# A two-layer scan kernel: carried states copied by VectorE instead of GpSimd, with three smaller edits

## The chip, the cores and the metric

The kernel runs on one core of a Trainium2 chip. Such a core has five engines with an instruction queue each: TensorE (PE in the profile), VectorE (DVE), ScalarE (ACT), GpSimd (POOL) and SyncE (SP, which here issues the transfers). Each engine works through its queue in order, and semaphores make an instruction wait for work on another engine. The metric is the device time of the whole launch in microseconds (us). The kernel before takes 21017.66 us, the median of three runs that lie between 21011.35 and 21024.16.

## The reference: two state-space layers

The input is a batch of 8 images of 48 x 48 positions with 192 channels. Each layer normalises it by groups, runs a selective scan over it, and adds the result to its input. Layer 0, which alone is changed, widens to 384 channels, runs a 3 x 3 convolution by channel, and scans every image in four directions `k`: by rows, by columns, and both of them backwards. Layer 1 scans single rows and columns forwards and backwards.

```python
xs = jnp.stack([xr, xc, jnp.flip(xr, -1), jnp.flip(xc, -1)], axis=1)
def step(h, inp):
    ut, dtt, bt, ct = inp
    dA = jnp.exp(dtt[..., None] * A)
    h = dA * h + (dtt * ut)[..., None] * bt[:, :, None, :]
    y = jnp.einsum('bkdn,bkn->bkd', h, ct)
    return (h, y)
y = ys[:, 0] + col2row(ys[:, 1]) + jnp.flip(ys[:, 2], -1) + col2row(jnp.flip(ys[:, 3], -1))
```

In words: for each of 384 channels and 16 states a first-order recurrence runs along 2304 positions. `dtt` is a softplus of a small projection, `bt` and `ct` are projections shared by the channels. The outputs of the four directions are added, normalised over the channels, multiplied by a gate `z`, and projected back to 192 channels.

## The kernel before

**Tiles.** The 384 channels are three groups `j` of 128 partitions. A direction's 2304 positions are cut into six chunks of 384. One chunk of one direction of one image is an *item*; layer 0 has 8 x 4 x 6 = 192 of them, and layer 1 as many. An item has 16 states `n` with three channel groups each, so 48 scan instructions of 128 x 384. The three scans of one state share a tile `h` of 128 x 1152; call them a *group*. Layer 0 has 3072 groups.

**One group on the engines.** ScalarE computes the decays `a = exp(dt * A)` (line 435), one per channel group. For most states a product `bT = dtu * B` is made, either by ScalarE in three instructions (line 464) or by GpSimd in one (line 459), and TensorE transposes it into a PSUM tile `b` (line 512, three banks in turn). For states 4 and 11 of layer 0 (`DIAGONAL`) a diagonal matrix `db` is made from B instead, by ScalarE in three instructions (line 483) or by GpSimd in one (line 480), and TensorE multiplies with it (line 503). For state 8 VectorE multiplies in PSUM (line 523). VectorE then scans: `h` from `a` and `b` (line 1059). GpSimd multiplies the whole `h` tile by `C`, in place (line 548, called the *gather* here). TensorE transposes and sums the result over the states into `y` (line 565). Four `h` tiles are in use in turn.

**The carried state.** A direction's chunks follow each other, so a scan starts from the last value of the chunk before it. After the three scans of a group, the last column of `h` (the first, for a reversed direction) is copied into a small tile `carry`, 128 x 3 elements (lines 541 to 544 ask for it, `put_carry`, line 1027, emits it, and the profile gives it line 1030). GpSimd does this copy immediately before its gather of the same tile, since the gather overwrites `h`. Every chunk but the last of a direction has it: 160 items x 16 = 2560 copies.

**What sets the order.** Nothing is scheduled at run time. Generators (`decays`, `weighs`, `matrices`, `places`, `scans`, `gathers`, `adds`, and others for the projections) yield a `Need`: a due time counted in scans, a cost for each engine that may do it, and what must precede it. `Plan.run` picks, with its own clock of assumed costs, the engine and the need that can start first, and among those ready the one due first; `late` adds to the due time on one engine. So an assumed cost decides which engine gets a step and where in that engine's queue it stands. Where only one engine has a cost, that engine always does it.

**Around the scans.** `enters` projects the items in pairs (due between `lo` and `hi`, in scans before the item's own) and `block` applies softplus to them. `products` forms `du = dt * u` on GpSimd (line 372). `finish` adds an item's output to `acc` on VectorE. `tails` normalises, gates and projects `acc` by chunks of eight rows, while the last direction of the image runs: after the add of the last direction's chunk `c`, it reads rows 8c to 8c + 7. In the kernel before, the last direction is `k = 3`, reversed columns, whose chunk `c` is eight columns over all rows.

Of the kernel before, what the change touches and what calls it, by code (L numbers as in the profile page):

```python
# [25 lines left out]
NJ = 3  # L26
# [7 lines left out]
NSEG = N * NJ  # L34
# [5 lines left out]
PE, DVE, ACT, POOL, SP = "PE", "DVE", "ACT", "POOL", "SP"  # L40
# [8 lines left out]
LATE = 3  # L49
# [34 lines left out]
class Plan:  # L84
# [11 lines left out]
    def mark(self, *key):  # L96
        return self.marks.setdefault(key, Mark())
# [85 lines left out]
class Common:  # L183
# [217 lines left out]
    def stream(self, plan, pool, items, direct, diagonal, decay, scan, finish, held, kept, weighed):  # L401
# [11 lines left out]
        nc, mark = self.nc, plan.mark  # L413
# [54 lines left out]
        def matrices():  # L468
            for i, item in enumerate(items):
                for n in sorted(diagonal):  # L470
                    after = [mark("bt", i)]
                    if placed:
                        after += [mark("place", placed[-1] + j) for j in range(NJ)]
                    need = Need(i * NSEG + NJ * n - 6, {POOL: 0.8, ACT: 0.72}, after, sets=[mark("matrix", i, n)])
                    yield need
                    to = dbs[i, n] = pool.tile([P, TB, P], F32, tag="db", name="db", bufs=1)
                    by = item["bt"][:, :, R + n : R + n + 1]
                    if need.e == POOL:
                        of = self.ident.unsqueeze(1).to_broadcast((P, TB, P))
                        nc.gpsimd.tensor_tensor(to, of, by.to_broadcast((P, TB, P)), ALU.mult)  # L480
                    else:
                        for b in range(TB):
                            nc.scalar.activation(to[:, b, :], self.ident, AF.Copy, scale=by[:, b, :])
                    placed.append(i * NSEG + NJ * n)
# [50 lines left out]
        def gathers():  # L535

            for f in range(total // NJ):
                i, n = divmod(f, N)
                item = items[i]
                after = [mark("scan", NJ * f + j) for j in range(NJ)]  # L540
                if "carry" in item:
                    need = Need(NJ * f + 2.5, {POOL: 0.15}, after, sets=[mark("carry", i, n)])
                    yield need
                    item["carry"](need.e, n, hs[f])
                yield Need(NJ * f + 3, {POOL: 2.6}, after + [mark("cc", i, n // 2)], sets=[mark("gather", f)])
                h = hs[f]
                c = ccs[i, n // 2][:, n % 2, :].unsqueeze(1).to_broadcast((P, NJ, T))
                nc.gpsimd.tensor_tensor(h, h, c, ALU.mult)  # L548
# [56 lines left out]
        for lane in (fetches, decays, weighs, matrices, places, scans, gathers, adds):  # L605
            plan.start(lane())
# [4 lines left out]
def layer0(ctx, cm, x, xs, x2, w, norm):  # L611


    tc, nc = cm.tc, cm.nc
# [3 lines left out]
    mark = plan.mark  # L618
# [22 lines left out]
    carry = wp.tile([P, N * NJ], F32, name="carry")  # L641
# [2 lines left out]
    vs = [cm.dram.tile([P, NJ, L], F32, name=f"v{b}") for b in range(NIMG)]  # L644
    per = 4 * NC
    span = per * NSEG

    def piece(b, c, due, tag="xc", bufs=2, after=(), of=x):
        n = Need(due, {SP: 0.1}, after, lag=DMA)
        yield n  # L650
        xc = pool.tile([CP, NM, T], F32, tag=tag, name="xc", bufs=bufs)
        nc.sync.dma_start(xc, of[b][:, :, c * T : (c + 1) * T])
        return xc, n
# [213 lines left out]
    def enters():  # L867

        last = len(items) // 2
        gated = []
        for p in range(last + 1):
            b, q = divmod(p, per // 2)
            g = 2 * p
            lo, mid, hi = g * NSEG - 92, g * NSEG - 50, g * NSEG - 32
            if q < 3 and p < last:
                lo, mid, hi = g * NSEG - 56, g * NSEG - 46, g * NSEG - 30
                if q == 0 and b:
                    n = Need(lo - 10, {SP: 0.3}, [mark("du", g - 1), mark("v", b)], lag=9.0)  # L880
                    yield n
                    for i in range(3):
                        part = slice(i * L // 3, (i + 1) * L // 3)
                        nc.sync.dma_start(u[:, :, part], vs[b][:, :, part])
                after = [n] if b else [mark("conv", j, c) for j in range(NJ) for c in (2 * q, 2 * q + 1)]
                if q == 0 or b == 0:
                    yield from block(lo, after, thirds=[(b, q)])
            if p < last:
                pair = items[g : g + 2]
                after = yield from cm.project(plan, pool, p, pair, lo, mid, hi)  # L890
                thirds = [(b, q + 1)] if q < 2 and b else []
            else:
                pair, after, thirds = [], [], []
            ended = [g - 2, g - 1] if p and (g - 2) % per >= 3 * NC else []
            for i in ended:
                n = Need(hi - 20, {SP: 0.1}, [mark("z used", gated[-2])] if len(gated) > 1 else [], lag=DMA)
                yield n
                zts[i] = pool.tile([P, NJ, T], F32, tag="z", name="z", bufs=2)
                bi, r = divmod(i, per)
                cs = slice((NC - 1 - r % NC) * T, (NC - r % NC) * T)  # L900
                nc.sync.dma_start(zts[i], zs[bi][:, :, cs])
                gated.append(i)
                after = after + [n]
            if pair or ended:
                yield from block(hi, after, pair, thirds, ended)

    def block(due, after, pair=(), thirds=(), ended=()):

        tables = 1 + bool(pair) + bool(thirds or ended)
        cost = tables * TABLE + 1.07 * len(pair) + 2.05 * len(thirds) + 1.07 * len(ended)  # L910
        sets = [m for i in pair for m in i["softened"]]
        sets += [mark("u", *t) for t in thirds] + [mark("silu z", i) for i in ended]
        yield Need(due, {ACT: cost}, after, sets=sets)
        cm.softplus(pair)
        for _, q in thirds:
            part = slice(q * L // 3, (q + 1) * L // 3)
            nc.scalar.activation(u[:, :, part], u[:, :, part], AF.Silu)
        for i in ended:
            nc.scalar.activation(zts[i], zts[i], AF.Silu)
        cm.tables()  # L920
# [90 lines left out]
    def seen(t, j, k, c):  # L1011

        t, q = t[:, j, :], "" if type(j) is int else "j "
        order = f"p {q}(h w) -> p {q}h w" if k % 2 == 0 else f"p {q}(h w) -> p {q}w h"
        return t.rearrange(order, w=S)[..., c * RT : (c + 1) * RT, :]

    def by_rows(v, k):

        return v.rearrange("p w h -> p h w") if k % 2 else v

    def wanted(b, k, c):

        if k:
            return []
        return [mark("tail", b - 1, c)] if b else [mark("free")]

    def put_carry(e, q, h, rev):
        to, of = carry[:, q * NJ : (q + 1) * NJ], h[:, :, 0 if rev else T - 1]
        if e == POOL:
            nc.gpsimd.tensor_copy(to, of)  # L1030
        else:
            nc.scalar.copy(to, of)

    items = []
    for b in range(NIMG):
        for k in range(4):
            rev = k >= 2
            order = range(NC - 1, -1, -1) if rev else range(NC)
            for n, c in enumerate(order):
                item = dict(  # L1040
                    b=b, k=k, c=c, reverse=rev, carried=(n > 0), A=A[:, k],
                    wts=dict(xp=xp[:, k], dtw=dtw[:, k, :], dtb=dtb[:, k, :]),
                    u=lambda j, k=k, c=c: by_rows(seen(u, j, k, c), k), turned=k % 2,
                    all=seen(u, slice(None), k, c),
                    ready=[mark("u", b, q) for q in ((c // 2,) if k == 0 else range(3))],
                    cost=(0.7, 3.1 if k % 2 else 2.6, 0.915),
                    wanted=lambda j, b=b, k=k, c=c: wanted(b, k, c),
                )
                item["softened"] = [mark("dt", len(items))]
                if n < NC - 1:  # L1050
                    item["carry"] = lambda e, q, h, rev=rev: put_carry(e, q, h, rev)
                items.append(item)
# [28 lines left out]

    plan.start(prologues())
    plan.start(enters())
    plan.start(tails())
    cm.stream(plan, pool, items, DIRECT[0], DIAGONAL[0], decay, scan, finish, 4, 9, 3)
# [349 lines left out]
```

## Time and profile before

| what | value |
|---|---|
| median of three runs | 21017.66 us |
| the profiled execution, its own time | 21021.07 us |
| its span, first to last instruction | 21019.3 us |
| mean granted TensorE clock | 0.996 |
| layer 0, first scan to the last chunk | 109 to 10515 us |
| layer 1, scans | 10609 to 20999 us |
| busy over the span: PE, DVE, ACT, POOL | 96%, 94%, 96%, 95% |
| DMA, mean rate | 72 GB/s, transfers 22.8% of the 16 engines' span |

Each profile row names a line of the kernel, an engine, an operation, the tiles it writes and reads, and the count; then busy time and the mean of one instruction in ns; then the idle time of the engine ahead of these instructions and whose work ended it. All four compute engines are busy nearly all the time, so a row's share of busy time does not by itself say what sets the end.

### The profile page before, as it was taken

The numbers are of one execution on the slowest core, as the hardware profiler recorded it, in microseconds if no ns is written. First come the engines' busy times: TensorE is split into PE (matmuls) and PEld (weight loads), VectorE is DVE, ScalarE is ACT, GpSimd is POOL, SyncE is SP. The second block draws the span as 40 slices with busy tenths as digits, with TensorE's granted clock in tenths as the row PEclk, the third lists the DMA queues.
The fourth block names the chain that finished last, engine by engine and source line by source line (L and its number), as shares of the span: only waits on it lengthen the run. The fifth ranks groups of instructions, "written<-read, shape, count | busy, mean of one in ns | idle before, by whom it ended". The sixth has DMA issues, their size and how long they took to land.

```text
span 21019.3 us, 391720 instructions
## 1 busy us (share of the span) xinstructions
PE 20233.5 (96%) x138640; PEld 15731.1 (75%) x138640; DVE 19835.8 (94%) x25014; ACT 20092.6 (96%) x38482; POOL 19933.6 (95%) x10537
## 2 busy tenths in 40 slices
PE   9999999999999999998899999999999999999999
PEld 6777777777777777777767777777777777777777
DVE  7999999999999999999989999999999999999999
ACT  7999999999999999999989999999999999999999
POOL 7999999999999999999989999999999999999999
PEclk9999999999999999999999999999999999999999
DMA  2222222222222222222222222222222222222222
GB/s 78 76 87 72 87 72 76 87 73 85 75 76 88 72 87 75 74 79 64 71 61 65 65 65 65 65 65 65 66 67 67 68 67 68 68 68 67 68 69 66
DMA packets 728906, 1512.36 MB, mean 72 GB/s; under 512 B 181508, under 2 KB 324484, under 8 KB 726824
## 3 DMA queue, kind: packets, MB, share of 16 engines
q1 hardware_dynamic: 724768, 1485.21, 22.8%
q8 instruction: 1106, 18.12, 0.4%
q14 instruction: 848, 6.95, 0.1%
q10 hardware_dynamic: 2184, 2.08, 0.0%
HBM read 1382.03 MB, written 104.99 MB: 71 GB/s over the span
## 4 chain that ended last, share of the span: by engine, by line
PE 57%; DVE 17%; ACT 10%; POOL 9%; issue 6%; DMA 1%; DVEq 0%; POOLq 0%; SPq 0%; ACTq 0%
PE y L565 18%; PE b L512 17%; DVE h L1298 9%; POOL h L548 7%; PE dt_ps L344 4%; ACT bT L464 3%; DVE h L1059 3%; PE xd_ps L295 3%; PE cv_ps L767 3%; PE b L503 2%; PE o_ps L1333 2%; ACT l_da L435 2%; ACT a L435 2%; PE xi_ps L1190 2%; PE z_ps L1240 2%
## 5 line engine op out<-in xcount | busy, mean ns | idle before, releaser
L548 POOL TENSOR_TENSOR h<-h,cc 128x1152 f32<-128x1152 f32 x6144 | 16177.2, 2647 | 719.3 <-DVE h L1298 257.5
L1298 DVE TENSOR_TENSOR_SCAN h<-l_da,b 128x384 f32<-128x384 f32 x9216 | 8110.6, 934 | 234.3 <-PE b L512 160.0
L565 PE MATMUL y<-ident,h 128*128 128x128 f32 x55296 | 7673.2, 275 | 188.9 <-POOL h L548 175.3
L512 PE MATMUL b<-ident,bT 128*128 128x128 f32 x48384 | 7402.7, 276 | 339.2 <-DVE h L1059 162.9
L1059 DVE TENSOR_TENSOR_SCAN h<-a,carry,b 128x384 f32<-128x384 f32 x7680 | 7201.6, 994 | 413.5 <-PE b L512 215.5
L464 ACT ACTIVATE bT<-dtu,bt 128x384 f32<-128x384 f32 x13026 | 7518.3, 606 | 54.9 <-PE b L512 45.5
L565 PEld LDWEIGHTS y<-ident,h 128*128 128x128 f32 x55296 | 6273.8, 141 | 1621.5 <-POOL h L548 708.2
L512 PEld LDWEIGHTS b<-ident,bT 128*128 128x128 f32 x48384 | 5557.4, 141 | 2022.0 <-issue 629.0
L435 ACT ACTIVATE a<-dt,l_A 128x384 f32<-128x384 f32 x9216 | 5282.5, 607 | 166.3 <-DVE h L1059 152.8
L435 ACT ACTIVATE l_da<-dt,l_A 128x376 f32<-128x376 f32 x9216 | 5107.6, 600 | 36.0 <-DVE h L1298 33.8
L459 POOL TENSOR_TENSOR bT<-dtu,bt 128x1152 f32<-128x1152 f32 x1034 | 2188.4, 2118 | 43.8 <-PE b L512 34.0
L1059 DVE TENSOR_TENSOR_SCAN h<-a,b 128x384 f32<-128x384 f32 x1536 | 1357.3, 936 | 131.3 <-PE b L512 73.2
L372 POOL TENSOR_TENSOR du<-dt,u 128x1152 f32<-128x1152 f32 x384 | 1072.2, 2792 | 148.6 <-ACT dt L360 139.8
L344 PE MATMUL dt_ps<-xd,l_dtw 12*128 12x384 f32 x2304 | 1039.6, 533 | 11.9 <-DVE dt L231 3.2
L295 PE MATMUL xd_ps<-u,l_xp 128*44 128x384 f32 x2304 | 959.2, 505 | 21.9 <-DVE z L1305 13.9
L767 PE MATMUL cv_ps<-pad,diag 128*128 128x384 f32 x2376 | 951.2, 488 | 0.0
L1240 PE MATMUL z_ps<-xt,l_z 96*128 96x384 f32 x2304 | 919.9, 490 | 16.5 <-DVE u L1215 11.2
L503 PE MATMUL b<-db,dtu 128*128 128x128 f32 x6912 | 925.1, 279 | 10.0 <-DVE h L1059 9.3
L1333 PE MATMUL o_ps<-z,l_out 128*96 128x384 f32 x2304 | 921.0, 488 | 5.7 <-DVE z L1305 5.0
L503 PEld LDWEIGHTS b<-db,dtu 128*128 128x128 f32 x6912 | 850.7, 193 | 83.7 <-DVE h L1059 42.4
L1190 PE MATMUL xi_ps<-xt,l_u 96*128 96x384 f32 x2304 | 894.8, 499 | 14.0 <-DMA l_z<-in_w_in 6.4
L1215 DVE SCALAR_TENSOR_TENSOR u<-xi_ps,l_conv_w,u 128x376 f32<-128x376 f32 (+1 forms) x1152 | 683.4, 593 | 43.4 <-ACT u L1209 22.2
(125 smaller groups left out, 14638.7 us busy)
## 6 DMA issues: line engine op xcount, KB each, us to landing
cc<-bc SPq DMA_DIRECT2D x3072, 384.0 KB, 3.5
xc<-in_x SPq DMA_DIRECT2D x186, 288.0 KB, 4.3
z<-v SPq DMA_DIRECT2D x144, 192.0 KB, 2.0
z<-z SPq DMA_DIRECT2D x48, 576.0 KB, 6.1
v<-v SPq DMA_DIRECT2D x126, 192.0 KB, 1.9
u<-v SPq DMA_DIRECT2D x21, 1152.0 KB, 9.1
xc<-in_xs SPq DMA_DIRECT2D x48, 288.0 KB, 4.2
x<-xc SPq DMA_DIRECT2D x48, 288.0 KB, 3.0
```

The lines of the kernel that those rows point to most:

```text
L295: nc.tensor.matmul(across(ps[:E, :T]), wts["xp"][:, j, :], item["u"](j), start=(j == 0), stop=(j == NJ - 1),)
L344: nc.tensor.matmul(ps[:, :T], wts["dtw"][:, j * P : (j + 1) * P], xd[:R, :], start=True, stop=True)
L435: nc.scalar.activation(dst, src, AF.Exp, scale=item["A"][:, j, n : n + 1])
L459: nc.gpsimd.tensor_tensor(to, of, by.to_broadcast((P, TB, DI)), ALU.mult)
L464: nc.scalar.activation(to[:, b, :], of[:, b, :], AF.Copy, scale=by[:, b, :])
L503: nc.tensor.matmul(ps[:, b * P : (b + 1) * P], item["dtu"][:, b, j * P : (j + 1) * P], dbs[i, n][:, b, :], start=True, stop=True,)
L512: nc.tensor.transpose(ps[:, b * P : (b + 1) * P], of, self.ident)
L548: nc.gpsimd.tensor_tensor(h, h, c, ALU.mult)
L565: nc.tensor.matmul(item["sum"][b][:, j * P : (j + 1) * P], hs[f][:, j, b * P : (b + 1) * P], self.ident, is_transpose=True, skip_group_che ...
L767: nc.tensor.matmul(rows(ps[:, :T]), diag[:, t, :], of[:, c * RT + t // 3 : (c + 1) * RT + t // 3, t % 3 : t % 3 + S], start=(t == 0), stop ...
L1059: nc.vector.tensor_tensor_scan(order(h[:, at % NJ, :]), order(a), order(b[:, :T]), carry[:, at : at + 1] if item["carried"] else 0.0, ALU. ...
L1298: nc.vector.tensor_tensor_scan(h[:, at % NJ, :], a, b[:, :T], 0.0, ALU.mult, ALU.add)
```

## The change

Five edits, all in layer 0:

1. The carried state is copied by VectorE, with an assumed cost of 0.1, instead of by GpSimd with 0.15. The place in the plan (due at 2.5 scans into the group) is the same.
2. For the diagonal matrix `db`, the assumed cost on ScalarE goes from 0.72 to 0.88, that on GpSimd from 0.8 to 0.78, and ScalarE's due time is set three scans later (`LATE`).
3. The first pair of items is due 60 scans sooner (`SOON`), both its projections and its `du`.
4. The two reversed directions change places, so the order of `k` is 0, 1, 3, 2. Reversed rows come last, and their chunk `c` is the eight rows that `tails` reads.
5. `put_carry` loses its ScalarE form.

```diff
-                    need = Need(i * NSEG + NJ * n - 6, {POOL: 0.8, ACT: 0.72}, after, sets=[mark("matrix", i, n)])
+                    need = Need(i * NSEG + NJ * n - 6, {POOL: 0.78, ACT: 0.88}, after, sets=[mark("matrix", i, n)], late={ACT: LATE})
...
                 if "carry" in item:
-                    need = Need(NJ * f + 2.5, {POOL: 0.15}, after, sets=[mark("carry", i, n)])
+                    need = Need(NJ * f + 2.5, {DVE: 0.1}, after, sets=[mark("carry", i, n)])
                     yield need
                     item["carry"](need.e, n, hs[f])
...
+    SOON = 60
...
                 lo, mid, hi = g * NSEG - 56, g * NSEG - 46, g * NSEG - 30
+                if p == 0:
+                    lo, mid, hi = lo - SOON, mid - SOON, hi - SOON
...
         to, of = carry[:, q * NJ : (q + 1) * NJ], h[:, :, 0 if rev else T - 1]
-        if e == POOL:
+        if e == DVE:
+            nc.vector.tensor_copy(to, of)
+        else:
             nc.gpsimd.tensor_copy(to, of)
-        else:
-            nc.scalar.copy(to, of)
...
-        for k in range(4):
+        for k in (0, 1, 3, 2):
...
+                    sooner=0 if items else SOON,
```

## The prediction

> **What bounds the kernel now.** I read the page's busy times first, then busy time by stage, then the groups, the waits, and two stretches of the timeline.
>
> ```profile
> PE 20233.5 (96%) x138640; PEld 15731.1 (75%) x138640; DVE 19835.8 (94%) x25014; ACT 20092.6 (96%) x38482; POOL 19933.6 (95%) x10537
> ```
>
> All four engines look full. By stage (columns: stretch, its length, then busy us of PE, PE loads, DVE, ACT, POOL):
>
> ```profile
> 30.00:90.00 60.00, 59.40 (x178) 32.44 (x178) 43.88 (x76) 19.28 (x30) 0.00 (x0) 1.00 0.14 41
> 109.00:10515.00 10406.00, 9927.49 (x69777) 7872.55 (x69776) 9696.81 (x11564) 9947.31 (x19404) 9964.56 (x6545) 0.99 0.25 78
> 10566.00:21019.00 10453.00, 10192.28 (x68516) 7796.64 (x68514) 10062.99 (x13306) 10091.65 (x18996) 9941.36 (x3946) 1.00 0.22 66
> ```
>
> The second line is layer 0: 10,406 us for 3,072 groups, 3.387 us a group. DVE is busy 9,697 of it, 3.157 a group, so it idles 0.23; POOL 95.8%, ACT 95.6%, PE 95.4%. No engine alone is the bound. In layer 0's waits the first by name are TensorE's `y` loads for POOL's gather (483 us) and DVE's scans for TensorE's `b` (289 us). Layer 1 shows how full such a pipeline gets: DVE 96.3%, PE 97.5%.
>
> The groups that the change touches:
>
> ```profile
> L548 POOL TENSOR_TENSOR h<-h,cc 128x1152 f32<-128x1152 f32 x6144 | 16177.2, 2647 | 719.3 <-DVE h L1298 257.5
> ...
> L1059 DVE TENSOR_TENSOR_SCAN h<-a,carry,b 128x384 f32<-128x384 f32 x7680 | 7201.6, 994 | 413.5 <-PE b L512 215.5 <-ACT a L435 41.7 <-PE b L503 40.5
> ...
> L1030 POOL COPY carry<-h 128x3 f32<-128x3 f32 x2560 | 487.8, 191 | 129.3 <-DVE h L1059 110.1 <-PE b L512 9.1 <-DVE gn L265 4.3
> ```
>
> POOL's timeline (start, length) gives the copy's true price there:
>
> ```profile
> 392.00 2.65 POOL L548 TENSOR_TENSOR h<-h,cc 128x1152 f32<-128x1152 f32 x1
> 394.58 0.19 POOL L1030 COPY carry<-h 128x3 f32<-128x3 f32 x1
> 394.85 2.64 POOL L548 TENSOR_TENSOR h<-h,cc 128x1152 f32<-128x1152 f32 x1
> ...
> 445.98 15.79 POOL L548 TENSOR_TENSOR h<-h,cc 128x1152 f32<-128x1152 f32 x6
> ```
>
> A gather with its copy takes 2.85 start to start (394.85 - 392.00); six gathers without it take 15.79, 2.63 each, and three elsewhere 7.80, 2.60 each. The copy costs POOL about 0.25.
>
> The decisive question is what it costs DVE. The group norm has tiny DVE instructions (96 x 2), among POOL's gathers:
>
> ```profile
> 1548.93 2.65 POOL L548 TENSOR_TENSOR h<-h,cc 128x1152 f32<-128x1152 f32 x1
> ...
> 1549.88 1.71 DVE L257 TENSOR_TENSOR gn_d<-gn_mv,gn_mean 96x2 f32<-96x2 f32 x1
> ...
> 1551.63 0.16 DVE L258 TENSOR_TENSOR gn_d<-gn_d 96x2 f32<-96x2 f32 x1
> 1551.79 2.61 POOL L548 TENSOR_TENSOR h<-h,cc 128x1152 f32<-128x1152 f32 x1
> 1551.82 2.60 DVE L259 TENSOR_TENSOR gn_d<-gn_d,gn_mv 96x2 f32<-96x2 f32 x1
> ```
>
> Line 257 starts inside a gather and ends with it (1551.59 against 1551.58). Line 258, between two gathers, takes 0.16. Line 259, 0.03 us after a gather's start, lasts as long as the gather. The reciprocal of the same size (line 272, one SBUF input) takes 0.142 on average and never over 0.163. So some DVE instructions stand until POOL's running instruction ends. Is a copy from SBUF to SBUF one of these? No such copy is in the trace; its nearest kin is a one-input instruction at the start, when POOL was idle (first window above):
>
> ```profile
> L839 DVE TENSOR_SCALAR u<-acc,l_conv_w,l_conv_b x8: 469/474/479, 40.5 to 87.0; 128x384 f32<-128x384 f32 x8
> ```
>
> Its rate tells how it reads. The form with a PSUM input and one scalar operand takes 606 (line 231), a plain PSUM copy 539 (line 224): an operand costs 67. Without its two, line 839 takes 340; less a fixed 150, 190 remain for 384 elements, 0.5 ns each. The PSUM copy needs (539 - 150) / 384 = 1.0 ns. Line 839 moves two elements at a time.
>
> **What the Trainium skill says.** "SBUF — State Buffer", section "Who interferes with whom": VectorE and GpSimd share one pair of SBUF ports under an exclusive lock; VectorE needs it with two SBUF inputs or in a two-port mode, and whoever comes second "fully blocks". For two inputs the trace agrees (above). "VectorE: DVE Perf Modes", section "Mode 2×_2P — use both read ports for one tensor": a single-source copy with both sides in SBUF takes this mode even in fp32, if the outermost count is even, or odd and equal on both sides. Line 839's rate agrees; the carried copy has 3 elements on both sides and would qualify. No run here shows that copy yet.
>
> **The change part by part.** Layer 1's instructions are the same in kind and number.
>
> *Copies leave POOL:* 2560 x 0.25 = 640 us. *Copies enter DVE:* in the order of the changed program, 2504 of 2560 stand directly behind their third scan. Own price: the 128 x 3 instructions at the start take 0.16 (lines 629 to 631), and a copy must wait for the scan ahead of it, which costs the 0.06 by which scans overlap (0.99 long, 0.93 start to start), less a little: 0.20. Not overlapping at all is the high end; the low end is 0.08 (reciprocal's 0.14 less 0.06).
>
> *The block.* If the copy needs the ports, it starts only when POOL's running instruction ends. Behind it in DVE's queue stand the next group's scans and the PSUM evacuations; TensorE waits for the scans after filling its three `b` banks. But the gather now waits for the copy, so POOL cannot run ahead: the two fall into step. Gather g starts 0.06 after copy g (as POOL now starts 0.06 after the scan that it waited for), and copy g+1 finds POOL idle if DVE's work was longer than POOL's. An interval thus takes the longer of DVE's work + 0.20 and POOL's + 0.06. A plain one is free: three scans 2.79 + 0.20 against 2.60 + 0.06. One with a `bT` (2.1), `du` (2.9) or `db` (0.8) behind the gather is not. I went through the changed order, interval by interval, with these durations and 0.5 for each of DVE's small instructions: DVE's work is 3.17 on average, the longer of the two 3.66 or 3.74, as POOL's extra work is counted with the gather after or before it; POOL is the longer in 651 or 667 intervals. So 3.70 a group. Of DVE's present idle 0.23 some stays, though the other engines then have slack (PE 3.23 of 3.8): I take half, 0.12, with 0 and 0.23 as ends. 3.82 - 3.387 = 0.43; x 2560 = 1,110 us. The 512 groups without a copy stay as they are.
>
> *Diagonal B:* 92 of these move, +92 x 0.834 = 77 us on POOL, -276 x 0.391 = -108 on ACT. The planner also moves 72 `bT` to POOL (72 x 2.118 = 152; ACT -216 x 0.606 = -131) and shifts evacuations between ACT (+18) and DVE (-20). POOL's net is -640 + 229 = -411, ACT's -221. Both are hidden under DVE; the moved `db` and `bT` are already in the interval sum, as longer POOL work. A `db` waits on POOL for TensorE's last use of its one buffer, holding the gather behind it: 4.0 us for 35 of them now, 15 us for 127.
>
> *First pair sooner:* the order of TensorE and ScalarE is the same up to the first scans, since softplus still waits for the convolutions; so 0. It could gain at most the 12 us between the softplus at 97 us and the first scan at 109. *Directions exchanged:* same counts, the strided adds cost 0.53 as others do: 0. Without that cover, a tail held by `acc` would cost its wait (DVE for TensorE's `o_ps`, 29 us in all).
>
> Sum against the profiled execution's own 21,021: +1,110 gives 22,131. The median of the runs is 3 us below that execution, so 22,130. With 3.66 and 0: +0.27 x 2560 = 690, 21,710; with 3.74 and 0.23: +1,490, 22,510. That is this case's own range.
>
> **The rivals.** (a) *The copy does not block* (it moves one element at a time, on DVE's own ports). Then DVE has 9,697 - 20 + 2560 x 0.08 to 0.20 = 9,882 to 10,189; at layer 1's 96.3% layer 0 takes 10,261 to 10,580, -145 to +174: 20,880 to 21,190. This is the way to a faster kernel; it decides at 0.135 a copy ((10,406 x 0.963 - 9,677) / 2560). For it: nothing shows such a copy blocked. Against: line 839. (b) *It blocks, at every copy, for the rest of a random POOL instruction*, as line 257 did on average (1.13, so 0.97 more): 3.36 + 0.97 - 3.387 = 0.94 x 2560 = 2,400, 23,420. For it: POOL is 95.8% busy. Against: the gather's wait for the copy. (c) *It blocks, but most waits replace DVE's idle time and POOL's extra work gets out of the copies' way*: 3.36 + 0.15 = 3.51, +0.12 x 2560 = 315, 21,330.
>
> **How the numbers follow.** Main case 0.60, (a) 0.11, (b) 0.14, (c) 0.15. The likeliest gives 22,130. From 21,300 to 23,250 the range holds the main case, nearly all of (c) and part of (b), leaving out (a) and the high half of (b), 0.18. No change within 0.2% (42 us) is what a measurement of this kernel can tell from none: (a) splits 0.06 faster, 0.03 same, 0.02 slower; all others are slower. A little is added to faster for what I don't see: 0.07, 0.03, 0.90.
>
> **What would show it.** The copy's row on DVE: a mean of some 0.5 us with a maximum near 2.1 to 2.9, against 0.14 to 0.2 throughout in (a) and over 1.1 in (b). POOL's gathers should idle for DVE, POOL and PE fall to about 85 to 88% in layer 0, and layer 1 keep its 10,450. If the copy's maximum stays under 0.3, the main case is wrong from the start.

## The result and the profile after

The changed kernel takes 21797.28 us (median of four runs, 21794.06 to 21804.44) against 21020.0 us for the kernel before on the same chip. The ratio is 1.0371, with a 95% interval from 1.0353 to 1.0389. The prediction said 22,130, in a range from 21,300 to 23,250: the direction and the main mechanism, the block, held, and the loss was overestimated, 1,110 us against some 777.

The page's busy line, after:

```profile
PE 20524.7 (94%) x138640; PEld 15821.2 (73%) x138640; DVE 20891.9 (96%) x27543; ACT 20081.1 (92%) x38021; POOL 19784.6 (91%) x8141
```

VectorE is busy 1,056 us more; TensorE, with the same instructions, 291 us more. By stage (stretch, its length, busy us, then the granted TensorE clock, the DMA share and GB/s), with the engines in the same order as before (PE, PE loads, DVE, ACT, POOL):

```profile
109.00:11290.00 11181.00, 10218.73 (x69812) 7962.13 (x69812) 10757.66 (x14099) 9937.00 (x18943) 9823.06 (x4147) 0.98 0.24 72
11345.00:21793.00 10448.00, 10188.76 (x68493) 7796.47 (x68491) 10058.30 (x13299) 10084.11 (x18989) 9937.82 (x3946) 1.00 0.22 66
```

Layer 1 is as it was (10,453 before). All of the loss lies in layer 0. From its first scan to the end of its last one it took 10,407 us before (109.0 to 10,515.6 in the trace) and takes 11,172 now (107.9 to 11,279.7): +765. VectorE is busy 1,057 us more in that stretch, and idle 292 us less. GpSimd is busy 146 us less (9,965 to 9,819), less than the 488 us of copies that left it, mainly because the planner gave it other work (228 us more of `bT` and `db`). TensorE's granted clock in layer 0 is 0.98, where it was 0.99. In the run with the sum below, where only the copy differs, it is 0.99 again, so the lower clock goes with the waits and is no cause of its own.

The groups that the change touches:

```profile
L548 POOL TENSOR_TENSOR h<-h,cc 128x1152 f32<-128x1152 f32 x6144 | 16161.9, 2644 | 1747.1 <-DVE carry L1033 867.6
...
L1064 DVE TENSOR_TENSOR_SCAN h<-a,carry,b 128x384 f32<-128x384 f32 x7680 | 7304.9, 996 | 175.2 <-PE b L512 66.5
...
L1033 DVE COPY carry<-h 128x3 f32<-128x3 f32 x2560 | 1178.4, 460 | 74.2
```

A copy of three elements has a mean of 460 ns on VectorE, where GpSimd took 191. GpSimd's gathers, which idled 719 us before, now idle 1,747, half of it for this copy. The copy's own row (shortest, median, longest) shows that the mean mixes two kinds of copy:

```profile
L1033 DVE COPY carry<-h x2560: 134/169/3212, 110.5 to 11227.4; 128x3 f32<-128x3 f32 x197
```

Half of the copies take 169 ns or less. In the trace 693 of the 2,560 take over 300, and their time beyond 169 sums to 735 us. A stretch of VectorE's timeline (start, length) shows both kinds:

```profile
3004.78 0.17 DVE L1033 COPY carry<-h 128x3 f32<-128x3 f32 x1
3004.86 2.82 DVE L1064 TENSOR_TENSOR_SCAN h<-a,carry,b 128x384 f32<-128x384 f32 x3
3007.72 0.17 DVE L1033 COPY carry<-h 128x3 f32<-128x3 f32 x1
...
3011.21 1.65 DVE L1033 COPY carry<-h 128x3 f32<-128x3 f32 x1
```

And GpSimd's timeline in the same stretch:

```profile
3002.16 2.63 POOL L548 TENSOR_TENSOR h<-h,cc 128x1152 f32<-128x1152 f32 x1 [0.16 <-POOL bT L459]
3005.12 2.64 POOL L548 TENSOR_TENSOR h<-h,cc 128x1152 f32<-128x1152 f32 x1 [0.33 <-DVE carry L1033]
3008.12 2.64 POOL L548 TENSOR_TENSOR h<-h,cc 128x1152 f32<-128x1152 f32 x1 [0.35 <-DVE carry L1033]
3010.72 2.11 POOL L459 TENSOR_TENSOR bT<-dtu,bt 128x1152 f32<-128x1152 f32 x1
3013.03 2.63 POOL L548 TENSOR_TENSOR h<-h,cc 128x1152 f32<-128x1152 f32 x1 [0.20 <-PE y L565]
```

The first two copies begin as a gather ends (3004.78 against 3002.16 + 2.63, 3007.72 against 3005.12 + 2.64) and take 0.17 us. GpSimd's next gather, which waits for the copy, starts 0.17 and 0.23 us after they end. The third comes 0.49 us after a `bT` has started, and ends (3012.86) as that `bT` does (3012.83). So it is for 678 of the 693 (the *held* copies below), which end within 0.05 us of the recorded end of the GpSimd instruction that ran when they began (0.025 in the median); the other 15 are held by the next one too. Counted by that instruction:

| GpSimd was at | copies held | waiting, us |
|---|---|---|
| `bT` | 246 | 325 |
| a gather | 239 | 186 |
| `du` | 132 | 186 |
| `db` | 41 | 18 |
| the tail's `acc`, `diag` | 35 | 19 |

Consecutive GpSimd records overlap a little (3008.12 + 2.64 against 3010.72 above), so some copies could be counted with the neighbour. Engines that need VectorE's scans wait longer too. In layer 0's waits (who waits, for whom: us in total, times, longest):

```profile
POOL h L548 <- DVE carry L1033: 867.6, 1641, 5.0
PEld b L512 <- DVE h L1064: 825.5, 1580, 3.2
ACT a L435 <- DVE h L1064: 748.4, 1177, 2.9
```

Before, TensorE's `b` loads and ScalarE's decays waited much less:

```profile
PEld b L512 <- DVE h L1059: 288.9, 661, 2.7
ACT a L435 <- DVE h L1059: 152.8, 317, 3.4
```

### The profile page after: what moved, and what is told of

It is laid out like the page before. It is cut to its first block, busy times and chain, and to the rows that moved or that the text cites. A ratio compares the mean times of both kernels' runs of the same rounds, so it can differ in the third digit from the quotient of the medians.

```text
span 21793.1 us, 392275 instructions
## 1 busy us (share of the span) xinstructions
PE 20524.7 (94%) x138640; PEld 15821.2 (73%) x138640; DVE 20891.9 (96%) x27543; ACT 20081.1 (92%) x38021; POOL 19784.6 (91%) x8141
## 4 chain that ended last, share of the span: by engine, by line
PE 55%; DVE 26%; ACT 9%; issue 6%; POOL 3%; DMA 0%; DVEq 0%; POOLq 0%; ACTq 0%; SPq 0%
PE b L512 17%; PE y L565 17%; DVE h L1064 11%; DVE h L1303 9%; PE dt_ps L344 3%; ACT bT L464 3%; PE xd_ps L295 3%; POOL h L548 3%; PE b L503 3%; PE cv_ps L768 3%; PE o_ps L1338 2%; ACT l_da L435 2%; PE xi_ps L1195 2%; ACT a L435 2%; PE z_ps L1245 2%
## 5 line engine op out<-in xcount | busy, mean ns | idle before, releaser
L512 PE MATMUL b<-ident,bT 128*128 128x128 f32 x48384 | 7656.3, 278 | 828.8 <-DVE h L1064 640.1
L565 PE MATMUL y<-ident,h 128*128 128x128 f32 x55296 | 7792.9, 276 | 121.6 <-POOL h L548 112.3
L464 ACT ACTIVATE bT<-dtu,bt 128x384 f32<-128x384 f32 x12810 | 7427.0, 605 | 108.7 <-PE b L512 94.1
L1064 DVE TENSOR_TENSOR_SCAN h<-a,carry,b 128x384 f32<-128x384 f32 x7680 | 7304.9, 996 | 175.2 <-PE b L512 66.5
L565 PEld LDWEIGHTS y<-ident,h 128*128 128x128 f32 x55296 | 6344.9, 142 | 1498.1 <-issue 694.1
L435 ACT ACTIVATE a<-dt,l_A 128x384 f32<-128x384 f32 x9216 | 5389.9, 607 | 785.4 <-DVE h L1064 748.4
L459 POOL TENSOR_TENSOR bT<-dtu,bt 128x1152 f32<-128x1152 f32 x1106 | 2338.4, 2116 | 64.0 <-PE b L512 46.5
L1033 DVE COPY carry<-h 128x3 f32<-128x3 f32 x2560 | 1178.4, 460 | 74.2
```

Source lines behind the costliest of these rows:

```text
L435: nc.scalar.activation(dst, src, AF.Exp, scale=item["A"][:, j, n : n + 1])
L459: nc.gpsimd.tensor_tensor(to, of, by.to_broadcast((P, TB, DI)), ALU.mult)
L464: nc.scalar.activation(to[:, b, :], of[:, b, :], AF.Copy, scale=by[:, b, :])
L512: nc.tensor.transpose(ps[:, b * P : (b + 1) * P], of, self.ident)
L565: nc.tensor.matmul(item["sum"][b][:, j * P : (j + 1) * P], hs[f][:, j, b * P : (b + 1) * P], self.ident, is_transpose=True, skip_group_che ...
L1064: nc.vector.tensor_tensor_scan(order(h[:, at % NJ, :]), order(a), order(b[:, :T]), carry[:, at : at + 1] if item["carried"] else 0.0, ALU. ...
```

## The experiments

The theory, as in the prediction: the copy reads two elements at a time, for which it needs the ports that GpSimd's instruction holds, and its waits are the loss. Rivals: any VectorE instruction from SBUF to SBUF would be held; the copy's own length and place cost it; one of the other edits does. "The trace" below is the profiled execution of each run.

### The edit alone, and everything but the edit

The kernel before, with only the copy moved:

```diff
-                    need = Need(NJ * f + 2.5, {POOL: 0.15}, after, sets=[mark("carry", i, n)])
+                    need = Need(NJ * f + 2.5, {DVE: 0.1}, after, sets=[mark("carry", i, n)])
...
-        if e == POOL:
-            nc.gpsimd.tensor_copy(to, of)
-        else:
-            nc.scalar.copy(to, of)
+        nc.vector.tensor_copy(to, of)
```

> The kernel before with one edit alone: the carried copy on VectorE at the assumed cost 0.1. Theory: this edit is the whole change of time, 21,650 to 21,950 us, mean row about 0.46 us and the same two-part distribution (most at 0.17, a quarter blocked). Rival (the moved diagonal B makes most of GpSimd's long stretches that block): under 21,500 us.

It took 21798.43 us, a ratio of 1.0373 (1.0357 to 1.0388): the changed kernel's time. Its row:

```profile
L1029 DVE COPY carry<-h x2560: 132/170/3193, 110.0 to 11242.0; 128x3 f32<-128x3 f32 x197
```

In its trace 686 copies wait 763 us. The reverse, the changed kernel with the copy back on GpSimd (the first line of the diff above turned round):

> The changed kernel with the carried copy alone given back to GpSimd at its old assumed cost; the other edits stay. Theory (the copies on VectorE, blocked by GpSimd, are the whole loss): back to 20,950 to 21,080 us, the copy's row on GpSimd at 0.19 us. Rival (the edits around it, diagonal B on GpSimd, the other order of directions, the earlier first pair, cost a part): more than 21,100 us, with the loss in layer 0 and no copy to blame.

It took 20993.53 us, a ratio of 0.9989 (0.9983 to 0.9996). Its row:

```profile
L1035 POOL COPY carry<-h x2560: 176/188/224, 111.8 to 10436.2; 128x3 f32<-128x3 f32 x197
```

So the copy's move is the whole loss. The other edits gain about 20 us together when the copy stays on GpSimd, and nothing that shows beside the blocked copies. Which of them gains was not tried.

### The same values moved one element at a time

The order of every instruction stays as in the changed kernel; the copy becomes a sum over one element:

```diff
-            nc.vector.tensor_copy(to, of)
+            at = 0 if rev else T - 1
+            nc.vector.tensor_reduce(to, h[:, :, at : at + 1], mybir.AxisListType.X, ALU.add)
```

> The changed kernel, every instruction in the same place, but the carried copy is written as a sum over one element per output, which moves the same 128 x 3 values through VectorE with one element read at a time. Theory (a two-element-a-step copy needs the ports that GpSimd holds): no row over 0.3 us, the 735 us of waiting go, and layer 0 comes to about (10,758 - 735) / 0.963 = 10,410 us, so 20,950 to 21,150 in all. Rival 1 (any VectorE instruction from SBUF to SBUF stands behind GpSimd): mean 0.46 us again and 21,750 to 21,850. Rival 2 (the copy's own length and its place between the scans cost it, not a block): 21,600 or more although no row is long.

It took 21105.92 us, a ratio of 1.0042 (1.0025 to 1.0059). Its row, and below it the first of layer 0's waits that name the copy:

```profile
L1034 DVE TENSOR_REDUCE carry<-h x2560: 130/157/164, 111.1 to 10545.2; 128x3 f32<-128x3 f32 x197
```

```profile
POOL h L548 <- DVE carry L1034: 431.8, 660, 5.0
```

No instruction of 2,560 is longer than 164 ns, although GpSimd is busy 9,773 of 10,489 us, and 1,358 of them began with over 0.3 us of a GpSimd instruction still to run. In the changed kernel's trace 632 copies began so, and 630 of them took over 0.3 us themselves. Engine, source, destination and place are the same, only the operation differs, and 691 us go. So the first rival falls, and the second explains at most the 0.0042 that is left. A second way to the same end cuts the copy into three copies of one element:

```diff
-            nc.vector.tensor_copy(to, of)
+            for j in range(NJ):
+                nc.vector.tensor_copy(to[:, j : j + 1], of[:, j : j + 1])
```

> The changed kernel with each carried copy cut into three copies of 128 x 1, the same kind of instruction with one element in place of three. Theory (the block belongs to reading two elements at a time, which one element can't do): no row over 0.3 us; three rows of about 0.15 us with overlap, some 0.08 us each beyond the first, so the one-element sum's 21,106 plus 2560 x 0.16 = 410 us at most: 21,250 to 21,550 us. Rival (the block belongs to the copy as an operation, whatever its length): a quarter of the first copies of each three still stand up to 3.2 us, 21,900 us or more.

```profile
L1034 DVE COPY carry<-h x7680: 117/144/158, 110.4 to 10546.0; 128x1 f32<-128x1 f32 x197
```

It took 21109.12 us, a ratio of 1.0044 (1.0029 to 1.0059). The operation is the copy again, and none is held, though 4,209 of the 7,680 began with over 0.3 us of a GpSimd instruction still to run: not every copy is blocked. This fits the theory, as one element can't be read as a pair; but how many elements the held copy reads at a time was not measured. It was also cheaper than expected. VectorE is busy 113 us more than with the sum (10,150 against 10,037), and the time is the same. VectorE's load alone was therefore not what set the end of these two kernels.

### What a second copy costs, and who is in step with whom

```diff
             nc.vector.tensor_copy(to, of)
+            nc.vector.tensor_copy(spare[:, q * NJ : (q + 1) * NJ], of)
```

> The changed kernel with every carried copy made twice, the second into a spare tile directly behind the first. Theory (in step: the gather waits for the copy, so GpSimd is mostly idle when a copy comes): the second copy mostly finds GpSimd still idle and adds its own price, 2560 x 0.13 to 0.17 = 330 to 440 us, or up to 700 us if another GpSimd instruction slips in between; 22,100 to 22,500 us. Rival (each copy meets a random part of a GpSimd instruction): the second waits as the first did on average, 0.46 us or more, so 1,180 us or more, 22,950 us or above.

It took 21972.52 us (ratio 1.0456, 1.0440 to 1.0471), 175 us over the changed kernel, half of the least expected. The second copy's row:

```profile
L1035 DVE COPY spare<-h x2560: 149/159/3233, 110.7 to 11413.4; 128x3 f32<-128x3 f32 x197
```

Its median is like the first one's, but 101 of 2,560 wait, not 693. So the second copy is mostly not held, as the theory said. It costs 0.07 us on the path (175 / 2560), less than its 0.16; overlap with its neighbour and VectorE's idle time would explain the rest, but no run takes them apart.

The prediction held that most copies go free because the gather waits for the copy. To take that wait away, the gather got a tile of its own to write. The run has two `h` tiles and two of the new ones in place of four `h`, and the order was planned for that (those lines are left out here):

```diff
-                nc.gpsimd.tensor_tensor(h, h, c, ALU.mult)
+                g = pool.tile([P, NJ, T], F32, tag="hc", name="hc", bufs=2) if kept == 9 else h
+                nc.gpsimd.tensor_tensor(g, h, c, ALU.mult)
+                hs[f] = g
```

> The changed kernel in which the gather writes a tile of its own, so that it no longer waits for the copy of the same group; h and the new tile have two buffers each, where h had four[...]. Theory (the gather's wait keeps the two engines in step and lets three of four copies through): now the gather starts as soon as the third scan ends, the copy behind the same scan meets it, and the copies' median goes from 0.17 to over 1 us, the mean to 1.3 us or more; 23,000 us or above. Rival (most copies are short because GpSimd happens to be idle, whatever waits for what): median 0.17 as before, time within 300 us of 21,797.

It took 22771.06 us (ratio 1.0834, 1.0814 to 1.0854):

```profile
L1039 DVE COPY carry<-h x2560: 149/169/6345, 109.6 to 12208.4; 128x3 f32<-128x3 f32 x197
```

This falls between the two: slower by almost 1,000 us, yet the median stays at 169 ns. With the smaller buffers in it, the run can't be read alone, so the same layout ran with the one-element sum:

> The run with the gather in a tile of its own, with the carried copy written as the one-element sum that does not block; every instruction in the same place. It prices the smaller buffers apart from the block. If the block's 1,205 us there are the whole rise above the unblocked 21,106, this takes 21,150 to 21,400 us. If the two-and-two buffers themselves cost the rest, 21,500 to 21,800 us.

```profile
L1040 DVE TENSOR_REDUCE carry<-h x2560: 134/157/164, 109.9 to 11111.6; 128x3 f32<-128x3 f32 x197
```

That took 21669.23 us (ratio 1.0311, 1.0281 to 1.0341). The layout itself thus costs 563 us over the unblocked 21,106, and the block in it 1,102 (22,771 - 21,669), against 691 in the changed kernel. The trace's own sums agree: 773 copies wait 1,205 us, and those behind gathers rise from 186 to 588 us. So the gather's wait for the copy limits the harm, but in this layout it is not why most copies are free. The trace shows the reason: GpSimd's gathers mostly begin 0.17 to 0.23 us after the third scan of their group, whose end releases both, and 1,646 of them begin before their copy has ended. The copy, mostly next in the scan's own queue, begins 0.03 us after the scan, and before its gather in 1,366 of these cases. It loses the race where another VectorE instruction stands between scan and copy: 278 copies found their own gather running and ended with it, and they wait 579 of the 1,205 us. These are what the gather's wait had prevented. One thing is not kept apart: with two `h` tiles the scans wait for the gather two groups back (286 us in the run with the sum), which can also keep the engines in step.

### Without GpSimd's other work

In layer 0 (`kept` is 9 there), ScalarE alone makes `bT` and `db`:

```diff
-                            costs[POOL] = 2.07
+                            if kept != 9:
+                                costs[POOL] = 2.07
...
-{POOL: 0.78, ACT: 0.88}
+{ACT: 0.88}
```

> The changed kernel with GpSimd freed of bT and diagonal B in layer 0, which ScalarE then makes alone (some 925 us more on ScalarE). Theory (what holds a copy is GpSimd's work beyond one gather): the 325 us behind bT and 18 us behind diagonal B go and nothing takes their place, so the copies' waiting falls from 735 to about 390 us and their mean to about 0.32 us; the time is ScalarE's then, 21,650 to 21,850 us. Rival (a copy meets whatever GpSimd runs, so gathers take the place): waiting stays above 600 us.

```profile
L1034 DVE COPY carry<-h x2560: 101/169/3270, 111.5 to 11244.1; 128x3 f32<-128x3 f32 x197
```

It took 21817.25 us (ratio 1.0381, 1.0351 to 1.0411). Only 314 copies wait, 298 us in all: the 343 us behind `bT` and `db` are gone, and the waits behind gathers fell too (186 to 99). `du` holds what it held, 186. ScalarE is now the busiest engine, 10,466 us in layer 0, but VectorE with its 10,443 us is close behind. That ScalarE's extra work is why the time didn't fall is an argument, not a thing shown.

### A version that beats both

The idea: unblocked, the copy is a load to be shared: odd states on VectorE as the sum, even states on GpSimd.

```diff
-need = Need(NJ * f + 2.5, {DVE: 0.1}, after, sets=[mark("carry", i, n)])
+need = Need(NJ * f + 2.5, {DVE: 0.14} if f % 2 else {POOL: 0.26}, after, sets=[mark("carry", i, n)])
```

> The changed kernel with the carried copy of odd states on VectorE, written as the one-element sum, and of even states on GpSimd; assumed costs 0.14 and 0.26. Theory (unblocked, the copy is only a load to be shared out: 0.137 us a piece on VectorE, 0.25 on GpSimd): VectorE about 9,690 + 1280 x 0.137 = 9,865 us busy in layer 0, GpSimd some 9,860; less than either whole form, 20,930 to 21,000 us. Rival (each kind of hand-over costs a wait of its own): between the two whole forms, 21,000 to 21,100 us.

It took 20967.97 us (9 runs), a ratio of 0.9975 to the kernel before (0.9965 to 0.9985): a quarter of a per cent, with the other edits in it. The rows:

```profile
L1036 POOL COPY carry<-h x1280: 176/189/262, 111.1 to 10405.9; 128x3 f32<-128x3 f32 x183
L1034 DVE TENSOR_REDUCE carry<-h x1280: 88/157/163, 118.0 to 10407.7; 128x3 f32<-128x3 f32 x183
```

VectorE is busy 9,840 us in its layer 0, GpSimd 9,816, ScalarE 9,888 and TensorE 9,924, of 10,352: the four are nearly level. Against the form with all copies on GpSimd (0.9989) it is ahead by 0.0014, some 29 us, though the two intervals overlap a little.

## Why the prediction was right, and where it was off

**The block.** That the copy would be held was inferred from line 839's rate, with a fixed 150 ns that was assumed, and from the Trainium skill's rule that a single-source copy within SBUF can take the two-port way ("VectorE: DVE Perf Modes", section "Mode 2×_2P — use both read ports for one tensor"). The block itself is shown: this trace has what no run had before, the 128 x 3 fp32 copy held until GpSimd's running instruction ends, as the Trainium skill says in "SBUF — State Buffer", section "Who interferes with whom". The sum and the one-element copies, which are not held, fit the two-port reading but do not measure it.

**The interval sum.** It had GpSimd as the longer in 651 or 667 intervals, and the longer of the two at 3.66 or 3.74 us against VectorE's 3.17 + 0.20: 0.29 to 0.37 us a group of waiting, some 740 to 950 us, of which the forecast took the middle, some 845. The trace has 693 held copies and 735 us, at the low end, so the pairing that counts GpSimd's extra work with the gather after it was the nearer one. That is 110 us of the excess. That the counts are so near is partly luck: 239 of the 693 stood behind a gather, and the sum took a plain interval for free. It also had 2,504 copies directly behind their third scan, where the trace has 2,160.

**The copy's own price.** This was the largest error. Taken: 0.20. VectorE's busy time rose by 1,057 us, of which 735 is waiting; with the 20 that left it for ScalarE, 342 / 2560 = 0.134 us. The row is 0.169, and it overlaps the scan behind it (3004.78 + 0.17 against 3004.86), which the forecast had left out. Excess 0.066 x 2560 = 170 us.

**VectorE's idle time.** Half of 0.23 was guessed to stay. Layer 0's idle fell from 709 to 417 us, 0.136 a group: right within 0.02. The rest of the excess, some 55 us, is VectorE's other work, taken as 3.17 a group, where the trace of before has 3.157, and 20 us of that went to ScalarE.

**Gather and copy in step.** The step "the gather now waits for the copy, so POOL cannot run ahead" was right as to the waits (868 us of them). As the reason for the free copies it was right only in part, as the run with the separate tile shows: there the median stayed, but 278 copies were held by their own gather. The hand-over was put at 0.06 us; it is 0.17 from copy to gather (3004.78 + 0.17 = 3004.95, gather at 3005.12; 0.17 also in the median). It is GpSimd's time and was hidden.

**The other edits.** Put at nothing: shown for all together (the edit alone gives the whole loss), with 20 us of gain when the copy is on GpSimd, which the forecast had not seen.

**The rivals.** Of (a) only the premise fell: its working for an unblocked copy, 20,880 to 21,190 (its figures give 20,870 for the low end), holds 21,106. But its limit, a VectorE full at 96.3%, is not the mechanism. Three one-element copies filled it to 96.8% at no cost. The sum's kernel is 112 us slower in layer 0 than the one with all copies on GpSimd, while GpSimd's gathers idle 432 us for the copy in it; whether that hand-over is the cost stays open. (b) fell: 73% of the copies are not held. (c), 21,330, underrates the waits, which were not absorbed: removing 735 us of them gave 691 back. Of the signs named ahead, the copy's mean (0.46 us, forecast some 0.5), GpSimd's share (88% of layer 0) and layer 1 came as forecast; the longest copy was longer (3.21 us), and TensorE fell to 91%, not 85 to 88%.

## What to carry to other kernels

Before a tiny instruction goes from one engine to another with time to spare, ask what it must hold in order to run, and whether a long instruction elsewhere holds it: the price of a 0.17 us copy can be the rest of a 2 to 3 us instruction. A few rows of a shared resource in the trace of before, here the tiny group-norm instructions that ended with a gather, are worth more than the average of any large group. And where an operation blocks, look for another form of the same step before giving the engine up: a sum over one element moved the same values without the wait.

## What the runs showed of the hardware that was not expected

- A copy with one element per partition (128 x 1) was never held in the run with three of them: 7,680 of them, none over 158 ns, with GpSimd busy 93% of layer 0. With three elements, 27% were.
- Three such copies (3 x 144 ns) cost the kernel no more time than one sum of 157 ns.
- A copy directly behind a scan on its own queue begins before GpSimd reacts to the same scan: where the gather does not wait for the copy, it begins 0.17 to 0.23 us after that scan's end in most cases, the copy 0.03 us after it.
- A copy of 0.17 us that begins in the last 0.15 us of a GpSimd instruction shows no wait: 930 of 941 such copies in the changed kernel took at most 176 ns, and the other 11 were held by the next instruction.
